# A two-layer graph network on one core: a fixed order ahead of the pairs, packed per-node scalars, and four blocks of counts kept as weights

## The chip, the cores and the metric

The kernel runs on one core of one Trainium2 chip. The metric is device time in microseconds, the median of several executions. The kernel before takes 452.44 us (three runs, 450.71 to 455.40); the profiled execution has a span of 452.8 us.

The core's engines are named as in the profile: PE is TensorE (matrix products), PEld its loading of weights, DVE is VectorE, ACT is ScalarE, POOL is GpSimd, SP only issues transfers.

## What is computed

`x` is 3327 x 64, `adj` is a symmetric 0/1 matrix of 3327 x 3327 with ones on its diagonal. Layer 0 works on every pair of nodes in hyperbolic space: for all i and j a logarithmic map of node j seen from node i, weighted by a sigmoid of two per-node logits and by the adjacency, summed over j; then per-node scalars, an exponential map and a projection. Layer 1 gives every edge the weight 0.5 to the power of the number of later edges in its row, for the last 100 edges of a row, and multiplies by a 64 x 64 weight.

```python
# layer 0, with h = relu(layernorm(x)); the result is added to x
x_t = logmap0(h, c)
left, right = x_t @ w_att[:D, 0], x_t @ w_att[D:, 0]
adj_att = sigmoid(left[:, None] + right[None, :] + b_att[0]) * adj
x_local = logmap(h[:, None, :], h[None, :, :], c)
support_t = einsum('ij,ijd->id', adj_att, x_local)
out = proj(expmap(h, support_t, c), c)
# layer 1, with h = relu(layernorm(x)) of the new x; the result is added to x
mask = adj != 0
rank = cumsum(mask, axis=1)
deg = rank[:, -1:]
k = minimum(deg, 100)
pos = rank - (deg - k)
w = mask * where(pos > 0, 0.5 ** (k - pos), 0)
out = w @ (h @ weight) + bias
```

The nodes are padded to 26 blocks of 128. The pairs are worked through in four strips of the i nodes (8, 8, 6 and 4 blocks wide); inside a strip a round is one block of j nodes (two blocks in the last strip), from the last j to the first. `NB` is 26, `P` 128, `D` 64.

## The kernel before

Ahead of the pairs, VectorE and ScalarE work out per-node scalars (`y`, `x2`, `nrm`, ...), features in float16 (`nz`, `nu`), their transposes (`jz`, `ju`) and the logits (`left`, `right`). The order of these instructions is left to a scheduler. All 26 blocks are transposed, in four groups:

```python
        for b0 in (24, 0, 16, 8):
            nb = min(8, NB - b0)
            for src, dst, rows in ((nu, ju, KB + 7), (nzf, jz, P)):
                pt = ps.tile([P, 8, P], F16, name="pq", bufs=2)
                for b in range(nb):
                    T.transpose(pt[:rows, b, :], src[:, b0 + b, :], id16)
                if dst is ju:
                    V.tensor_copy(dst[:rows, b0 : b0 + nb, :], pt[:rows, :nb, :])
                else:
                    A.copy(dst[:rows, b0 : b0 + nb, :], pt[:rows, :nb, :])
    ...
        for b in (*range(16, NB), *range(16)):
            for part in (0, 1):
                T.matmul(plr[:, b, :], jz[:, b, :], w_h[:, part], start=part == 0, stop=part == 1)
        V.tensor_mul(left, plr[:, :, 0], yr)
        V.tensor_mul(right, plr[:, :, 1], yr)
        V.tensor_scalar(right, right, batt, 0.5, op0=ALU.add, op1=ALU.mult)
    ...
        V.tensor_mul(hw[:, :, D], opx, wn)
        V.tensor_mul(wn, wn, y)
        for hs in node_halves[::-1]:
            V.tensor_mul(hw[:, hs, :D], rl[:, hs], wide(wn[:, hs], 13))
        V.tensor_mul(h, rl, wide(y, NB))
        V.tensor_scalar(balm, bal, MIN_NORM, None, op0=ALU.max)
        V.tensor_mul(su, nrm, balm)
        V.tensor_mul(sv, bal, su)
```

The pairs, whose order on TensorE, VectorE and ScalarE is that of the program:

```python
        queue = nc.scalar if k == 0 else nc.sync
        iz = strip.tile([P, 8, P], F16, name="iz")[:, :nb]
        iu = strip.tile([KB, 8, P], F16, name="iu")[:, :nb]
        queue.dma_start(iu[:D], ju[:D, blocks])
        queue.dma_start(iu[D:], ju[KB : KB + 7, blocks])
        queue.dma_start(iz[:D], jz[D:, blocks])
        queue.dma_start(iz[D:], jz[:D, blocks])
    ...
        kept = behind(j)[:, S.i0 : S.i0 + S.F]
        num, den = ON_ACT[k]
        i = NB - 1 - j
        if (n < AHEAD and k == 0) or i * num // den != (i + 1) * num // den:
            A.activation(kept, S.pc[:, : S.F], AF.Relu)
        else:
            V.tensor_scalar(kept, S.pc[:, : S.F], 0.0, None, op0=ALU.max)
    ...
    def strip_out(k):
        S = strips[k]
        S.ot = work.tile([P, FMAX], F32, name="sg", bufs=SGB)[: D + 1]
        V.tensor_copy(S.ot[:, : S.F], S.po[: D + 1, : S.F])
    ...
    steps = range_steps()
    strip_in(0)
    for n in range(AHEAD + 2):
        load(n)
    for n in range(AHEAD + 1):
        edges(n)
    for n in range(AHEAD):
        for j in js(n):
            count(n, j)
            read(n, j)
    with tc.manual_schedule(engines=IN_ORDER):
        products(0)
        for n in range(R):
            k, lo, hi = rounds[n]
            m, w = n + AHEAD, span(n)
            ended, turned = (n > i and rounds[n - i - 1][1] == 0 for i in (1, 2))
            if m + 2 < R:
                if rounds[m + 2][2] == NB:
                    strip_in(rounds[m + 2][0])
                load(m + 2)
            two = m < R and len(js(m)) == 2
            if two:
                count(m, js(m)[0])
            if turned:
                pa = turn(k - 1)
            elif n > 1:
                total(n - 2)
            pq = pq_of.pop(n)[:, :w]
            A.activation(pq, pq, AF.Gelu, scale=-WG / QS)
            A.activation(pq, pq, AF.Gelu, scale=WH)
            if n == 0:
                first_left()
                sigmoids(0)
            elif n == 1:
                left_to_dram()
            asked_of_act()
            if turned:
                steps = per_node(k - 1, pa)
            sg = sg_of[n][:, :w]
            V.scalar_tensor_tensor(sg, sg, 1.0, ad_of.pop(n)[:, :w], op0=ALU.add, op1=ALU.mult)
            if m + 1 < R:
                edges(m + 1)
            if two:
                read(m, js(m)[0])
            if m < R:
                count(m, js(m)[-1])
            if n + 1 < R:
                sigmoids(n + 1)
            if m < R:
                read(m, js(m)[-1])
            if n + 1 < R:
                products(n + 1)
            if hi - lo > 1:
                advance(PORTIONS[k])
            V.scalar_tensor_tensor(sg, pq, WD, sg, op0=ALU.add, op1=ALU.mult)
            if ended:
                strip_out(k - 1)
            advance(PORTIONS[k])
            if lo == 0:
                for _ in steps:
                    pass
                asked = False
            if turned:
                total(n - 2)
        total(R - 2)
        total(R - 1)
        strip_out(len(STRIPS) - 1)
        steps = per_node(len(STRIPS) - 1, turn(len(STRIPS) - 1))
```

`edges` makes a bfloat16 mask of the adjacency, `count` adds the edges behind every edge in PSUM, and `read` keeps these counts as bytes in `behind_lo` or `behind_hi`. `sigmoids`, `products` and `total` are the tanh of the logits, the pair products and the sum over j. The per-node tail of a strip (`post`) is a generator: in the first three strips its small instructions go to GpSimd, in the last to VectorE, and `yield` gives the share of a round that a step takes; `LATER` ends the round's share and `ACT` asks ScalarE for the next step. In the profile, L1064 and L1065 are the two Gelu of a round, L1075 the product with the adjacency, L1090 the final product, L974 a count read by VectorE, L1120 and L1122 the decodes of ScalarE and VectorE, and L849 the first large instruction that needs the tail's scalars (`V.tensor_mul(w, hs, ...)`). A shortened view of `post`:

```python
        def after(slots):
            for do, args, kwargs in asked_of_w:
                do(*args, **kwargs)
                if not hidden:
                    yield 1
            asked_of_w.clear()
            if not hidden:
                pass
            elif nb > 6:
                yield from [LATER] * slots
            else:
                yield from [LATER] * (slots + slots // 2)
        def root(y, v):
            t = small("rs_t")
            if hidden:
                W.tensor_tensor(y, v, nhalf[:, :nb], op=ALU.pow)
                W.tensor_mul(t, y, y)
                W.tensor_mul(t, t, v)
                W.tensor_scalar(t, t, -0.5, 1.5, op0=ALU.mult, op1=ALU.add)
                W.tensor_mul(y, y, t)
            else:
                rsqrt(W, pool, y, v, nb)
        ...
        A.activation(u, v, AF.Square)
        V.tensor_mul(dt, hs, v)
        yield BIG
        V.tensor_reduce(hv, dt, AX.X, ALU.add)
        yield BIG
        V.tensor_reduce(vv, u, AX.X, ALU.add)
        yield BIG
        muladd(sa, hv, m2c, agg[:, :, D])
        mul(sa, sa, su[:, bs])
        mul(xy, hv, sv[:, bs])
        mul(t0, sa, x2[:, bs])
        W.tensor_sub(xy, xy, t0)
        mul(u2, vv, sv[:, bs])
        mul(t0, sa, hv)
        W.tensor_sub(u2, u2, t0)
        mul(u2, u2, sv[:, bs])
        mul(t0, sa, xy)
        W.tensor_sub(u2, u2, t0)
        W.tensor_scalar(t0, u2, MIN_NORM, None, op0=ALU.max)
        root(rn, t0)
        mul(t0, t0, rn)
        mul(t0, t0, sk[:, bs])
        yield from after(2)
        yield ACT
        A.activation(k, t0, AF.Tanh)
        yield 0
        scaled(k, k, absr, rn)
        ...  # some 25 small instructions, one reciprocal, and a second root
        yield from after(4)
        V.tensor_mul(w, hs, wide(t0, nb))
        yield BIG
        ...  # 8 more large ones, and a third root
```

Layer 1 turns the counts, shifted by 7 bits, into bfloat16 weights by reading them as exponents (`decode`), and sums over j in seven PSUM banks:

```python
        def decode(j):
            wt = l1.tile([P, NP], U16, name="wt", bufs=7)
            if j % 2:
                A.activation(wt, behind(j), AF.Copy, scale=128.0)
            else:
                V.tensor_scalar(wt, behind(j), 128.0, None, op0=ALU.mult)
            return wt
        ...
        for j in range(late):
            wt = decode(j)
            asked_of_act()
            advance(LAST)
            if j == 8:
                in_range(l1_ps)
            for n in range(len(chunks)):
                add(j, wt, n)
            if j % 4 == 3:
                bias(j - 3, 4)
        for _ in steps:
            pass
        bias(late - 2, 2)
        bias(late, NB - late)
        weights = [decode(j) for j in range(late, NB)]
    ...
        for n in range(len(chunks)):
            for j in range(late, NB):
                add(j, weights[j - late], n)
            if n % 2:
                A.copy(ow[n], pw[n])
            else:
                V.tensor_copy(ow[n], pw[n])
            if n > 1:
                close(n - 2)
        close(len(chunks) - 2)
        close(len(chunks) - 1)
```

Of the kernel before, what the change touches and what calls it, by code (L numbers as in the profile page):

```python
# [22 lines left out]
P = 128  # L23
# [7 lines left out]
JH = 13  # L31
IN_ORDER = {mybir.EngineType.PE, mybir.EngineType.DVE, mybir.EngineType.Activation}
AHEAD = 3
SGB, ADB = 5, 7
# [3 lines left out]
PORTIONS, LAST = (2, 4, 4, 8), 8  # L38
BIG, LATER, ACT = 4, 99, 100

# [402 lines left out]
def fast(ctx, tc, x, adj_t, r, w_att, b_att, weight, bias, out, flag):  # L443
# [76 lines left out]
    def wide(t, n):  # L520
# [3 lines left out]
    h = const.tile([P, NB, D], F32, name="h")  # L524
    x2, bal, balm, nrm, left, right, sv, su, sk = (
        const.tile([P, NB], F32, name=n)
        for n in ("x2", "bal", "balm", "nrm", "left", "right", "sv", "su", "sk"))
# [4 lines left out]
    behind_hi = const.tile([P, NB - JH, NP], U8, name="behind_hi")  # L532
# [5 lines left out]
    pairs = ctx.enter_context(ExitStack())  # L538
    ps = pairs.enter_context(tc.tile_pool(name="ps", bufs=1, space=PSUM))

    with tc.tile_pool(name="pre", bufs=1) as pre:
        def small(name):
            return pre.tile([P, NB], F32, name=name)


        d, rl, sq, sr = (pre.tile([P, NB, D], F32, name=n) for n in ("d", "rl", "sq", "sr"))
        m, ss, rs, y, v = (small(n) for n in ("m", "ss", "rs", "y", "v"))
        for hs in node_halves:
            n = hs.stop - hs.start
            V.tensor_reduce(m[:, hs], x_sb[:, hs], AX.X, ALU.add)  # L550
            V.scalar_tensor_tensor(d[:, hs], wide(m[:, hs], n), -1.0 / D, x_sb[:, hs], op0=ALU.mult, op1=ALU.add)
            A.activation(sq[:, hs], d[:, hs], AF.Square)
            A.activation(rl[:, hs], d[:, hs], AF.Relu)
            A.activation(sr[:, hs], rl[:, hs], AF.Square)
        for hs in node_halves:
            V.tensor_reduce(ss[:, hs], sq[:, hs], AX.X, ALU.add)
            V.tensor_reduce(rs[:, hs], sr[:, hs], AX.X, ALU.add)
        V.tensor_scalar(v, ss, 1.0 / D, EPS_LN, op0=ALU.mult, op1=ALU.add)
        rsqrt(V, pre, y, v, NB)
        V.reciprocal(inv_r, r_c)  # L560
        V.tensor_mul(c_c, inv_r, inv_r)
        V.tensor_scalar(negc, c_c, -1.0, None, op0=ALU.mult)
        V.scalar_tensor_tensor(sqc, inv_r, -1.0, inv_r, op0=ALU.mult, op1=ALU.max)
        V.tensor_scalar(zs_c, sqc, ZS, None, op0=ALU.mult)
        V.tensor_scalar(za_c, c_c, -0.5 * ZS, None, op0=ALU.mult)

# [659 lines left out]
```

## Time and profile before

| engine | busy us | share of the span | instructions |
|---|---|---|---|
| TensorE | 371.7 | 82% | 1438 |
| VectorE | 383.3 | 85% | 579 |
| ScalarE | 371.5 | 82% | 410 |
| GpSimd | 95.7 | 21% | 231 |

| stage | us from the span's start |
|---|---|
| first final product of a pair round (L1090) starts | 50.2 |
| strip 1's first L1090 | 140.9 |
| strip 2's first L1090 | 239.7 |
| strip 3's first L1090 | 327.3 |
| last sums of the pairs copied (L1004) | 385.1 |
| last decode of layer 1 ends | 434.4 |
| last VectorE instruction ends | 445.4 |

No engine is full over the whole span, and three are close to it together; so the shares say little, and the stages have to be read one by one. Times of waits are what an engine stood idle before an instruction, put down to what released it last.

### The profile page before, as it was taken

Reading aid. Unit: us, or ns where it says so; the run is one execution under the profiler, and the core shown is the slowest. Engines: PE = TensorE matmul, PEld = TensorE weight load, DVE = VectorE, ACT = ScalarE, POOL = GpSimd, SP = SyncE. Lnnn points to the kernel's source line nnn. Section 1 sums busy time; section 2 is a strip of 40 time slices with the busy share of each in tenths; the row PEclk is TensorE's granted clock in tenths of the full one; section 3 lists DMA queues with packets and bytes.
Section 4 is the critical chain, followed back from the end, with each engine's and each line's share of the span. In section 5 each row is a group of like instructions: output and inputs, shape, how many; then the busy total and the mean of one; then the engine's idle time right before and its main releaser. Section 6 shows DMA issues by size and latency. Waiting matters only on the chain.

```text
span 452.8 us, 4738 instructions
## 1 busy us (share of the span) xinstructions
PE 371.7 (82%) x1438; PEld 159.3 (35%) x1460; DVE 383.3 (85%) x579; ACT 371.5 (82%) x410; POOL 95.7 (21%) x231
## 2 busy tenths in 40 slices
PE   0436899999997999989997999697979958768963
PEld 0124333333333333333333444343333312323443
DVE  3893799999999899799999686999999776989821
ACT  1645999999999899979998799699998946893940
POOL 5000000000000257702400468023026812000000
PEclk9997799999999899989998899699999979899997
DMA  8503344544547345344345353336534000000002
GB/s 194 211 1 73 121 159 140 167 154 144 157 142 226 109 147 165 94 139 137 106 125 162 83 150 117 96 114 186 160 120 139 0 0 0 1 1 0 1 23 60
DMA packets 23313, 48.98 MB, mean 108 GB/s; under 512 B 8714, under 2 KB 9170, under 8 KB 23280
## 3 DMA queue, kind: packets, MB, share of 16 engines
q1 hardware_dynamic: 20993, 47.66, 35.0%
q10 hardware_dynamic: 2062, 0.87, 1.0%
q0 software_dynamic: 224, 0.07, 0.3%
q8 instruction: 13, 0.21, 0.2%
q14 instruction: 21, 0.16, 0.1%
HBM read 46.40 MB, written 0.87 MB: 104 GB/s over the span
## 4 chain that ended last, share of the span: by engine, by line


## 5 line engine op out<-in xcount | busy, mean ns | idle before, releaser
L998 PE MATMUL po<-sg,hw 128*65 128x512 f32 (+1 forms) x364 | 164.2, 576 | 1.6 <-DVE sg L1090 1.5
L1090 DVE SCALAR_TENSOR_TENSOR sg<-pq,sg 128x1024 f32<-128x1024 f32 (+1 forms) x91 | 103.7, 1139 | 8.6 <-ACT pq L1065 8.3
L1075 DVE SCALAR_TENSOR_TENSOR sg<-sg,ad 128x1024 f32<-128x1024 f32 (+1 forms) x91 | 103.7, 1139 | 7.0 <-ACT sg L981 6.7
L981 ACT ACTIVATE sg<-left_b,right 128x1024 f32<-128x1024 f32 (+2 forms) x104 | 100.5, 980 | 0.0
L1064 ACT ACTIVATE pq<-pq 128x1024 f32<-128x1024 f32 (+1 forms) x91 | 87.1, 957 | 7.1 <-PE pq L989 6.2
L1065 ACT ACTIVATE pq<-pq 128x1024 f32<-128x1024 f32 (+1 forms) x91 | 86.2, 947 | 2.9
L961 PE MATMUL pc<-mask,ca 128*128 128x512 bf16 (+1 forms) x169 | 64.8, 383 | 24.4 <-DVE behind_lo L974 11.7
L998 PEld LDWEIGHTS po<-sg,hw 128*65 128x65 f32 x364 | 50.8, 141 | 74.5 <-issue 60.8
L962 PE MATMUL pc<-mask,cb 128*128 128x512 bf16 (+1 forms) x170 | 63.9, 385 | 15.9 <-DVE mask L950 13.9
L989 PE MATMUL pq<-iz,jz 128*128 128x512 f16 (+1 forms) x182 | 67.9, 379 | 4.0 <-DMA iz<-jz 4.0
L988 PE MATMUL pq<-iu,ju 71*128 71x512 f16 (+1 forms) x182 | 69.5, 382 | 1.0 <-DVE sg L1090 0.3
L950 DVE TENSOR_SCALAR mask<-ad 128x1024 bf16<-128x1024 f32 (+1 forms) x91 | 59.2, 652 | 0.6 <-PE pc L961 0.6
L1127 PE MATMUL pw<-wt,s 128*128 128x512 bf16 (+1 forms) x178 | 41.7, 383 | 9.2 <-DVE wt L1122 5.5
L962 PEld LDWEIGHTS <-cb 128*128 128x128 bf16 x182 | 18.5, 101 | 78.5 <-issue 61.6
L755 POOL TENSOR_SCALAR sa<-hv,m2c 128x8 f32<-128x8 f32 (+1 forms) x3 | 3.0, 1004 | 201.5 <-ACT behind_hi L972 147.9
L972 ACT ACTIVATE behind_lo<-pc 128x1024 uint8<-128x1024 f32 (+2 forms) x32 | 27.4, 855 | 12.2 <-PE pc L962 6.8
L972 ACT ACTIVATE behind_hi<-pc 128x1024 uint8<-128x1024 f32 (+2 forms) x31 | 27.0, 871 | 8.1 <-PE pc L962 8.1
L1127 PEld LDWEIGHTS <-s 128*128 128x128 f16 x182 | 18.4, 103 | 30.5 <-issue 13.0
L961 PEld LDWEIGHTS <-ca 128*128 128x128 bf16 x175 | 17.9, 102 | 30.6 <-issue 19.5
L989 PEld LDWEIGHTS <-jz 128*128 128x128 f16 x182 | 18.6, 102 | 24.8 <-issue 4.5
L988 PEld LDWEIGHTS <-ju 71*128 71x128 f16 x182 | 18.6, 102 | 24.6 <-DVE sg L1090 4.7
L1132 POOL TENSOR_TENSOR x_sb<-x_sb,bias_b 128x256 f32<-128x256 f32 (+1 forms) x7 | 7.2, 1042 | 79.5 <-DVE w L860 79.5
(265 smaller groups left out, 346.6 us busy)
## 6 DMA issues: line engine op xcount, KB each, us to landing
ad<-in_adj_t SPq DMA_DIRECT2D x65, 512.0 KB, 3.6
ad<-in_adj_t SPq DMA_DIRECT2D x26, 384.0 KB, 3.2
out<-o SPq DMA_DIRECT2D x6, 128.0 KB, 2.6
left_b<-left_d SPq DMA_DIRECT2D x1, 512.0 KB
x_sb<-in_x ACTq DMA_DIRECT2D x1, 416.0 KB, 5.7
x_sb<-in_x SPq DMA_DIRECT2D x1, 416.0 KB, 5.1
left_b<-left_d SPq DMA_DIRECT2D x1, 384.0 KB, 4.2
iz<-jz SPq DMA_DIRECT2D x2, 128.0 KB, 2.7
```

Of the source, the lines that this page charges most:

```text
L950: V.tensor_scalar(*args, 0.0, None, op0=ALU.not_equal)
L961: T.matmul(S.pc[:, f0:f1], ca, S.before[:, f0:f1], start=False, stop=True, skip_group_check=True)
L962: T.matmul(S.pc[:, f0:f1], cb, now[:, f0:f1], start=S.first, stop=True, skip_group_check=True)
L981: A.activation(part(n, sg, j), S.left[:, : S.F], AF.Tanh, bias=right[:, j : j + 1], scale=0.5)
L988: T.matmul(part(n, pq, j, f0, f1), ju[:KB, j, :], S.iu[:, f0:f1], start=True, stop=False)
L989: T.matmul(part(n, pq, j, f0, f1), jz[:, j, :], S.iz[:, f0:f1], start=False, stop=True)
L998: T.matmul(S.po[: D + 1, f0:f1], hw[:, j, :], part(n, sg_of[n], j, f0, f1), start=j == NB - 1, stop=j == 0)
L1064: A.activation(pq, pq, AF.Gelu, scale=-WG / QS)
L1065: A.activation(pq, pq, AF.Gelu, scale=WH)
L1075: V.scalar_tensor_tensor(sg, sg, 1.0, ad_of.pop(n)[:, :w], op0=ALU.add, op1=ALU.mult)
L1090: V.scalar_tensor_tensor(sg, pq, WD, sg, op0=ALU.add, op1=ALU.mult)
L1127: T.matmul(pw[n], s2[:, j].rearrange("p c d -> p (c d)"), wt[:, f0:f1].bitcast(BF16), start=j == 0, stop=j == NB - 1)
```

## The change

It has five parts.

1. *A fixed order ahead of the pairs.* The part ahead of the loop also gets a written order on TensorE, VectorE and ScalarE. The blocks that the first rounds need (0 to 7 and 24, 25) are transposed first, the first strip's regrouping transfers are issued by SP and GpSimd, not ScalarE, and what is needed later (the other blocks, the weights `hw`, scalars of the tail) moves into the first two rounds. Two rounds are counted ahead, not three, and there are five adjacency buffers, not seven.
2. *Packed per-node scalars.* In the tail, scalars that go through the same operation are neighbours in one tile, so that one instruction does both; `h` is no longer kept (`hw` times a per-node factor `ih` stands in). The last strip's roots take a power on GpSimd in place of three refinement steps on VectorE. The waiting steps are given as times and divided by a round's length (`ROUND`).
3. *Counts kept as weights.* Blocks 12 to 15 (`JD`) are written by `read` as 16-bit weights at once and need no decode; layer 1 begins with them.
4. *One decode ahead.* The first decode is asked for ahead of the last strip's tail; a tail that isn't done at the end of its strip goes on in the next stage.
5. *The range test in the loop.* The test that decides whether the general path must run moves from layer 1 into the last two rounds. The copy of a strip's sums is split between VectorE and ScalarE, and stands ahead of the round's final product.

The diff, cut to its core:

```diff
-JH = 13
+JD = range(12, 16)
 IN_ORDER = {mybir.EngineType.PE, mybir.EngineType.DVE, mybir.EngineType.Activation}
-AHEAD = 3
-SGB, ADB = 5, 7
+AHEAD = 2
+SGB, ADB = 5, 5
 ON_ACT = ((1, 2), (5, 8), (3, 4), (1, 2))
-PORTIONS, LAST = (2, 4, 4, 8), 8
+PORTIONS, LAST = (2, 4, 4, 8), 6
 BIG, LATER, ACT = 4, 99, 100
+ROUND = (3.5, 3.5, 2.8, 1.9)
...
+    for n in range(AHEAD + 2):
+        load(n)
+    pairs.enter_context(tc.manual_schedule(engines=IN_ORDER))
...
+    first_i, last_j, later = slice(0, 8), slice(24, NB), slice(8, 24)
...
+    p1 = ps.tile([P, 16, P], F16, name="pq", bufs=2)
+    turned_to(p1, first_i, 0)
+    p2 = ps.tile([P, 4, P], F16, name="po")
+    turned_to(p2, last_j, 0)
+    kept(p1, first_i, 0)
+    strip_in(0)
+    kept(p2, last_j, 0)
+    p3 = ps.tile([P, 16, P], F16, name="pq", bufs=2)
...
+    logits((first_i, last_j))
+    products(0)
+    rest(later)
+    high, low = slice(16, 24), slice(8, 16)
+    turned_to(p3, high, 0)
+    pl = first_left()
+    products(1)
+    edges(AHEAD)
+    pq = pq_of[0]
+    A.activation(pq, pq, AF.Gelu, scale=-WG / QS)
+    A.activation(pq, pq, AF.Gelu, scale=WH)
+    kept(p3, high, 0)
+    strips[0].left, left_b = pl, strips[0].left
+    sigmoids(0)
+    A.copy(left_b[:, : strips[0].F], pl[:, : strips[0].F])
+    strips[0].left = left_b
...
+    def last_of_ahead():
+        p4 = ps.tile([P, 16, P], F16, name="po")
+        turned_to(p4, low, 0)
+        kept(p4, low, 0)
         wn, opx = small("wn"), small("opx")
         V.tensor_scalar(wn, nrm, WA / 2, None, op0=ALU.mult)
         V.tensor_scalar(opx, x2, c_c, 1.0, op0=ALU.mult, op1=ALU.add)
         V.tensor_mul(hw[:, :, D], opx, wn)
         V.tensor_mul(wn, wn, y)
-        for hs in node_halves[::-1]:
-            V.tensor_mul(hw[:, hs, :D], rl[:, hs], wide(wn[:, hs], 13))
-        V.tensor_mul(h, rl, wide(y, NB))
+        V.tensor_mul(hw[:, 13:, :D], rl[:, 13:], wide(wn[:, 13:], 13))
+        yield
+        logits((later,))
+        left_to_dram()
+        yield
+        V.tensor_mul(hw[:, :13, :D], rl[:, :13], wide(wn[:, :13], 13))
+        V.tensor_scalar(ih, babs, 2 / WA, None, op0=ALU.mult)
...
+            A.activation(kept, S.pc[:, : S.F], AF.Relu, scale=128.0 if j in JD else 1.0)
+        elif j in JD:
+            V.tensor_scalar(kept, S.pc[:, : S.F], 0.0, 128.0, op0=ALU.max, op1=ALU.mult)
...
+        other = nc.gpsimd if k == 0 else nc.sync
+        iz = strip.tile([P, 8, P], F16, name="iz")[:, :nb]
+        iu = strip.tile([KB, 8, P], F16, name="iu")[:, :nb]
+        other.dma_start(iz[:D], jz[D:, blocks])
+        nc.sync.dma_start(iz[D:], jz[:D, blocks])
+        other.dma_start(iu[:D], ju[:D, blocks])
+        nc.sync.dma_start(iu[D:], ju[KB : KB + 7, blocks])
...
+        def power(y, v, exponent):
+            asked_of_w.append((G.tensor_tensor, (y, v, exponent[:, :nb]), {"op": ALU.pow}))
+        def root(y, v):
+            power(y, v, nhalf)
+            mul(rt, y, y)
+            if hidden:
+                mul(rt, rt, v)
+                W.tensor_scalar(rt, rt, -0.5, 1.5, op0=ALU.mult, op1=ALU.add)
+                mul(y, y, rt)
+            else:
+                W.scalar_tensor_tensor(rt, v, -0.5, rt, op0=ALU.mult, op1=ALU.mult)
+                W.scalar_tensor_tensor(y, rt, 1.5, y, op0=ALU.add, op1=ALU.mult)
...
+                    yield LATER if kwargs.get("op") == ALU.pow else 1
             asked_of_w.clear()
-            if not hidden:
-                pass
-            elif nb > 6:
-                yield from [LATER] * slots
-            else:
-                yield from [LATER] * (slots + slots // 2)
-        def root(y, v):
-            t = small("rs_t")
             if hidden:
-                W.tensor_tensor(y, v, nhalf[:, :nb], op=ALU.pow)
-                W.tensor_mul(t, y, y)
-                W.tensor_mul(t, t, v)
-                W.tensor_scalar(t, t, -0.5, 1.5, op0=ALU.mult, op1=ALU.add)
-                W.tensor_mul(y, y, t)
-            else:
-                rsqrt(W, pool, y, v, nb)
-        hs, v, xs = h[:, bs], agg[:, :, :D], x_sb[:, bs]
-        sa, t0, t1, k, y2, u2, xy, hv, vv, rn = (
-            small(n) for n in ("sa", "t0", "t1", "k", "y2", "u2", "xy", "hv", "vv", "rn"))
-        u, w, dt = big("u"), big("w"), big("dt")
+                yield from [LATER] * math.ceil(time / ROUND[k + 1])
...
+        mul(d, dots[:, 1:], both(of_sum[:, 1]))
+        mul(e, dots[:, :2], both(of_sum[:, 0]))
+        W.tensor_sub(d, d, e)
+        mul(e, d, of_sum)
+        W.tensor_sub(d[:, 1], e[:, 1], e[:, 0])
...
-        V.tensor_copy(S.ot[:, : S.F], S.po[: D + 1, : S.F])
+        for f0, f1 in S.hv:
+            if f0 == 0:
+                V.tensor_copy(S.ot[:, f0:f1], S.po[: D + 1, f0:f1])
+            else:
+                A.copy(S.ot[:, f0:f1], S.po[: D + 1, f0:f1])
...
+        if ended:
+            strip_out(k - 1)
+        if 0 < n < R - 1:
...
+        if n > R - 3:
+            next(range_end)
...
+    order = [*JD, *range(JD.start), *range(JD.stop, late)]
...
+            nonlocal decoded
+            if j in JD:
+                return behind(j)
             wt = l1.tile([P, NP], U16, name="wt", bufs=7)
-            if j % 2:
+            decoded += 1
+            if decoded % 2:
...
+        weights = {j: decode(j) for j in order[: len(JD) + 1]}
+        stages.append(Stage(per_node(len(STRIPS) - 1, pa)))
...
```

## The prediction

> **What bounds the kernel now.** The chain that ended last is empty on this page, so I read stage by stage: first the busy time of each engine in stretches, cut where the strips change.
>
> ```profile
> core 0: us, PE busy (x) PEld busy (x) DVE busy (x) ACT busy (x) POOL busy (x), PEclk, DMA share, GB/s
> 0.00:50.00 50.00, 18.19 (x134) 11.72 (x136) 31.01 (x103) 24.99 (x30) 6.57 (x26) 0.93 0.38 109
> 50.00:140.00 90.00, 89.27 (x301) 33.95 (x306) 89.86 (x100) 88.43 (x91) 0.00 (x0) 0.98 0.53 162
> 140.00:239.00 99.00, 92.41 (x312) 35.44 (x316) 92.92 (x101) 93.46 (x101) 34.77 (x68) 0.97 0.45 133
> 239.00:327.00 88.00, 77.06 (x313) 36.33 (x316) 76.95 (x103) 78.29 (x106) 29.08 (x68) 0.92 0.45 132
> 327.00:385.00 58.00, 47.34 (x146) 16.99 (x147) 46.72 (x56) 45.52 (x65) 24.55 (x68) 0.94 0.19 55
> 385.00:435.00 50.00, 37.38 (x164) 16.79 (x167) 40.79 (x110) 39.10 (x18) 0.73 (x1) 0.93 0.00 1
> ```
>
> The stretches are the front, strips 0 to 3, and layer 1 up to its last decode; the close takes the remaining 18 us. Strip 0 is full: VectorE 89.9 of 90 us, ScalarE 88.4. There a round takes 2.87 us on VectorE without a count read and 4.00 with one, 3.43 on average, and nothing short of less work helps. Strips 1, 2 and 3 leave VectorE idle for 6, 11 and 11 us, layer 1 for 9. The list of waits for VectorE says what ended most of that:
>
> ```profile
> DVE w L849 <- POOL t L755: 11.2, 3, 4.4
> DVE sg L1090 <- ACT pq L1065: 8.3, 12, 1.9
> DVE sg L1075 <- ACT sg L981: 6.7, 1, 6.7
> ```
>
> The first line is the per-node tail: in each of strips 1 to 3 VectorE stops once, for 3.2, 3.6 and 4.4 us, for scalars that GpSimd is still working out. The third is the first round, which waits for the chain ahead of the pairs. In the timeline of VectorE and then in four stretches after it, the third GpSimd wait shows what it costs besides itself:
>
> ```profile
> 363.45 0.56 DVE L849 TENSOR_TENSOR w<-h,t 128x384 f32<-128x384 f32 x1 [4.36 <-POOL t L755]
> ```
>
> ```profile
> 366.00:370.00 4.00, 1.32 (x3) 0.56 (x4) 3.93 (x7) 0.49 (x1) 0.46 (x1) 0.75 0.00 0
> 370.00:374.00 4.00, 4.00 (x7) 1.24 (x6) 2.04 (x3) 2.86 (x5) 0.68 (x2) 0.50 0.00 0
> ```
>
> TensorE has 1.3 us of work in one stretch, and in the next it runs with a granted clock of 0.50. In layer 1 the timeline of ScalarE shows which decodes come last:
>
> ```profile
> 405.26 2.96 ACT L1120 ACTIVATE wt<-behind_hi 128x3328 uint16<-128x3328 uint8 x1
> 413.99 0.42 ACT L863 ACTIVATE dt<-w 128x256 f32<-128x256 f32 x1 [5.76 <-DVE w L860]
> 414.31 2.96 ACT L1120 ACTIVATE wt<-behind_hi 128x3328 uint16<-128x3328 uint8 x1
> 419.61 0.40 ACT L874 CAST s<-w 128x256 f16<-128x256 f32 x1 [2.34 <-DVE w L871]
> 419.92 14.44 ACT L1120 ACTIVATE wt<-behind_hi 128x3328 uint16<-128x3328 uint8 x5
> ```
>
> Thirteen decodes of 2.9 us sit on ScalarE, which stops 5.8 and 2.3 us for the last strip's per-node work on VectorE and ends at 434.4. TensorE's last 28 products need that decode, so the 11 us of closing begin there.
>
> [...] a wait of 5.3 us, then clock 0.50. [...] here GpSimd's 128x8 scale took 0.20 to 0.28 us in some places and 1.75 in others[...]. [...] a 128x4 product takes 0.16 us here and 128x256 takes 0.42, so packing two 128x4 products into one saves almost all of one. [...]
>
> **The change part by part.**
>
> *Front.* Before, the first final product (L1090) starts at 50.16. The chain that sets it: features at 25.6, transposed and copied in four groups up to 37.9, the DMA regrouping of the first strip issued from 32.8 but landed only at 42.7 (half of it sits in ScalarE's queue behind copies and the table load), then the activations. The change transposes just the needed ten blocks first and moves those DMAs to two other queues. Walking the new program order with the durations of this page: x can start at about 6.5 (before it waited behind the r scalars until 8.2), per-node scalars end at 21, the first features at 22.5, transposes at 27, DMA landed at 31, first products at 33. But `left` needs the logarithms (32.4), and its transposes stand in TensorE's order behind a group that waits for the later blocks (38), so the first tanh is at 40.5 and the first L1090 at about 44: 6 us sooner. Against that stand postponed items, now in rounds 0 and 1, where VectorE has no room: two weight copies of 0.95, one ju copy 0.6, and some twenty small ones of about 0.15: 5 us. The 1.9 us `h` product disappears, but it was ahead. I book a net -2.
>
> *One look-ahead less.* Two rounds counted ahead instead of three: one mask (0.6) and half of a read (1.14) move into full rounds, +1.
>
> *GpSimd's scalars.* Packed chains are shorter (the middle one has 33 instructions for 38, and it took 19 us before), and slots are now sized by time: 16 us at 3.5 us a round gives 5 rounds where 4 were waited. In strips 2 and 3 it is 6 and 9 steps for 4 and 6. I expect all 11.2 us to go. All of it is on the path, because VectorE and ScalarE are both full between the strips.
>
> *After the third wait.* With TensorE warm, the last four rounds need not take 17.4 us (364.40 to 381.84 between L1090s); ScalarE's floor for a round without a count is 3.2 us (375.68 to 378.86), 12.8 for four: -4.
>
> *Strip ends.* The copy of the sums is issued before L1090 (1.14 us earlier) and halved with ScalarE. TensorE waited 2.8 us plus 2.5 us for it at two strip ends and 0.8 at the last, and VectorE 1.3 and 1.9 behind that: -3.
>
> *Layer 1.* TensorE needs 26 x 6.5 x 0.213 us = 36 us at full clock (its start-to-start distance is about 0.21), so the decodes and the last strip's scalars bind. Two decodes fewer per engine: 3.6 us of VectorE (1.81 start to start), 5.8 of ScalarE. The range test leaves (1.6 us). Small VectorE instructions fall from 76 to 46: at some 0.17 us each, 5. Back come three GpSimd powers of 1.35 us, half covered by a decode (+3), and the rest of strip 2's post that no longer ends inside strip 3 (5 large instructions, +2.5). VectorE was packed from 385.75 to 428.9, 43 us: 43 - 3.6 - 1.6 - 5 + 3 + 2.5 = 38. ScalarE needs 11 x 2.9 plus 2.5 = 34.5 and again waits for VectorE. Its last decode, 49 us after the pairs before, should come at 41: -8. I don't take the 12 us that TensorE's own floor would allow.
>
> Sum: -2 + 1 - 11.2 - 4 - 3 - 8 = -27, and 452.4 - 27 = 425.
>
> **Rivals.** (1) *The front gives nothing or costs.* A fixed order loses what the scheduler filled in; the postponed work meets full engines. For it: strip 0 has no slack. Against it: 6.7 us of idle VectorE ahead of the first round. That makes 430 or so. (2) *A load wait takes the place of the GpSimd wait.* Seven adjacency buffers become five, so from release to use there are two rounds, 6.9 us, not three. A load lands in 3.6 us, but at each strip's start 0.9 MB of regrouped features stand in front of it in the same queue. Against it: the DMA share is 0.5 and no load wait shows now. If it binds, about 1 to 3 us at three places: 428 to 434. (3) *Layer 1 stays bound by the chain through VectorE,* with GpSimd's powers put into it: then that part gives 3 and not 8, 430. (4) *Better:* TensorE's floor in layer 1 is reached and the front chain is shorter than I walked it: 414.
>
> **Range and chances.** The certain core is the 11 us of GpSimd waits and the two decodes per engine; 9 us, the 2% line, is less than the first alone. Front and layer 1 are each uncertain by 5 or 6 us, the strip ends by 3, together about 9. So 425, 413 to 440; faster 0.91, same 0.06, slower 0.03.
>
> **What would show it.** The wait of L849's successor on GpSimd near zero; L1090's first start near 44, and rounds 0 to 2 longer than 4 us; no granted clock near 0.5 in strip 3; the last decode about 41 us after the pairs end. Wrong would be: VectorE waiting for loads at strip starts, a first L1090 later than 48, or ScalarE still pausing 8 us in layer 1.

## The result and the profile after

| | before | after |
|---|---|---|
| time, median of four executions | 452.62 us (450.71 to 455.40) | 436.23 us (435.56 to 436.67) |
| ratio, 95% interval | | 0.963 (0.958 to 0.968) |
| span of the profiled execution | 452.8 us | 434.5 us |

So 16.4 us were gained, and 27 had been booked: 436.2 lies in the range, 11 us above the 425 of the prediction. Between the two profiles it is 18.3, because the profiled execution of the kernel before took 454.5 us, 2 us above its median; the differences between stages below contain these 2 us. First the stages of the kernel after, with the cuts moved to its own strips; columns as in the same view of the kernel before.

```profile
core 0: us, PE busy (x) PEld busy (x) DVE busy (x) ACT busy (x) POOL busy (x), PEclk, DMA share, GB/s
0.00:45.00 45.00, 14.12 (x98) 8.66 (x98) 28.10 (x87) 22.79 (x29) 8.49 (x30) 1.00 0.32 90
45.00:142.00 97.00, 92.12 (x343) 35.63 (x344) 95.90 (x122) 91.28 (x93) 0.19 (x1) 0.96 0.52 158
142.00:237.00 95.00, 91.46 (x317) 34.70 (x315) 91.61 (x100) 92.44 (x100) 35.13 (x62) 0.98 0.46 140
237.00:317.00 80.00, 72.42 (x313) 34.28 (x312) 73.70 (x101) 76.80 (x104) 33.41 (x62) 0.98 0.48 138
317.00:374.00 57.00, 48.83 (x155) 17.44 (x153) 49.40 (x66) 48.52 (x66) 22.58 (x52) 0.94 0.25 74
374.00:415.00 41.00, 33.34 (x163) 15.69 (x163) 33.18 (x74) 31.44 (x17) 11.60 (x11) 1.00 0.00 1
```

The front is 5 us shorter (45 for 50), but strip 0 is 7 us longer (97 for 90), strips 1 and 2 are 4 and 8 us shorter, strip 3 hardly. VectorE is again full in strip 0 and idle for 3, 6 and 8 us in strips 1 to 3. In its list of waits, what was first is gone and two waits are new (the final product is now L1173, the product with the adjacency L1154, the decodes L1205 and L1207, a strip's aggregates, its sums turned back to one node per partition, are copied half by L1098 on ScalarE and half by L1100 on VectorE, where before ScalarE copied both halves; the large product that needs the tail's scalars is L1045):

```profile
DVE agg L1100 <- ACT agg L1098: 5.7, 3, 2.0
...
DVE w2s L1190 <- DMA w<-in_weight: 4.2, 1, 4.2
DVE rt_last L967 <- POOL rn_last L967: 2.7, 3, 0.9
...
DVE w L1067 <- POOL rn L967: 0.5, 1, 0.5
```

No line has L1045: the 11.2 us of waits for GpSimd have become 0.5 (L1067, a later step of the tail), and in layer 1 three short waits for the new powers come to 2.7. New is the first line: three times, once in each of strips 1 to 3, VectorE's half of the aggregates' copy waits about 2 us for ScalarE's half, and stands ahead of everything VectorE would do next. At the start of strip 3 this is what follows, in the timeline of TensorE and in the two stretches around it:

```profile
328.29 0.59 PE L629 MATMUL pc<-mask,ca 128*128 128x512 bf16 x1 [4.19 <-DVE behind_hi L644]
```

```profile
325.00:329.00 4.00, 0.71 (x2) 0.25 (x2) 3.35 (x6) 1.80 (x4) 0.00 (x0) 0.76 0.14 19
329.00:333.00 4.00, 4.00 (x8) 1.39 (x7) 3.69 (x5) 2.93 (x4) 2.97 (x8) 0.50 0.32 116
```

VectorE reads a count late, TensorE waits 4.2 us for the free buffer, and then runs at a granted clock of 0.50 (called cold below). The four rounds there take 5.28, 6.73, 6.10 and 4.50 us; the kernel before took 3.67, 5.39, 3.94 and 3.90 in its own. Layer 1 on ScalarE:

```profile
369.05 2.97 ACT L1205 ACTIVATE wt<-behind_lo 128x3328 uint16<-128x3328 uint8 x1
374.77 0.38 ACT L1098 COPY agg_last<-po 128x260 f32<-128x260 f32 x1 [2.75 <-PE po L1088]
...
380.05 0.51 ACT L1070 CAST s<-w 128x384 f16<-128x384 f32 x1 [4.17 <-DVE w L1067]
...
405.50 0.40 ACT L1070 CAST s<-w_last 128x256 f16<-128x256 f32 x1 [3.05 <-DVE w_last L1067]
405.81 8.70 ACT L1205 ACTIVATE wt<-behind_hi 128x3328 uint16<-128x3328 uint8 x3
```

The last decode (the end of the last line) is at 414.5, 41.0 us after the last copy of the sums begins (373.53; before it was 49.2), though ScalarE pauses for 11.0 us on the way (2.75, 4.17, 3.05 in these lines, 0.63 and 0.41 in others).

Cut at the first final product of each strip, the two profiles give this account; the booked terms are the prediction's.

| stage | before | after | booked | found |
|---|---|---|---|---|
| start to strip 1 | 140.89 | 141.87 | -2 + 1 | +1.0 |
| strip 1 | 98.77 | 95.27 | | -3.5 |
| strip 2 | 87.63 | 80.06 | | -7.6 |
| strip 3, to its last final product | 54.55 | 53.08 | | -1.5 |
| strips 1 to 3 together | | | -11.2 - 4 - 3 | -12.5 |
| last final product to last decode | 52.52 | 44.24 | -8 | -8.3 |
| last decode to the end | 18.41 | 19.96 | 0 | +1.5 |

Layer 1 is as booked. Missing are 5.7 us in the strips, 2 in the front and 1.5 in the closing. The experiments ask for each.

### The profile page after: what moved, and what is told of

Read it like the earlier page. It is cut to its first block, busy times and chain, and to the rows that moved or that the text cites. A ratio compares the mean times of both kernels' runs of the same rounds, so it can differ in the third digit from the quotient of the medians.

```text
span 434.5 us, 4704 instructions
## 1 busy us (share of the span) xinstructions
PE 364.4 (84%) x1460; PEld 155.8 (36%) x1460; DVE 377.1 (87%) x556; ACT 365.0 (84%) x409; POOL 111.4 (26%) x218
## 4 chain that ended last, share of the span: by engine, by line
DVE 38%; ACT 23%; PE 22%; issue 10%; POOL 3%; DMA 2%; POOLq 0%; DVEq 0%; ACTq 0%
DVE sg L1173 11%; DVE sg L1154 10%; PE po L668 8%; ACT sg L651 6%; ACT pq L1147 5%; DVE behind_lo L644 3%; ACT pq L1148 3%; PE pc L629 2%; PE pq L658 2%; PE pq L659 2%; PE pc L630 2%; DVE wt L1207 2%; ACT wt L1205 2%; DVE behind_hi L644 2%; ACT behind_lo L640 2%
## 5 line engine op out<-in xcount | busy, mean ns | idle before, releaser
L668 PE MATMUL po<-sg,hw 128*65 128x512 f32 (+1 forms) x364 | 161.1, 566 | 0.4 <-DVE st L895 0.4
L1173 DVE SCALAR_TENSOR_TENSOR sg<-pq,sg 128x1024 f32<-128x1024 f32 (+1 forms) x91 | 103.8, 1140 | 6.6 <-ACT pq L1148 5.3
L1154 DVE SCALAR_TENSOR_TENSOR sg<-sg,ad 128x1024 f32<-128x1024 f32 (+1 forms) x91 | 103.9, 1142 | 2.5 <-ACT sg L651 2.4
L651 ACT ACTIVATE sg<-left_b,right 128x1024 f32<-128x1024 f32 (+2 forms) x103 | 99.5, 978 | 1.0 <-DVE right L819 1.0
L1147 ACT ACTIVATE pq<-pq 128x1024 f32<-128x1024 f32 (+1 forms) x90 | 86.1, 957 | 4.4 <-PE pq L659 4.3
L1148 ACT ACTIVATE pq<-pq 128x1024 f32<-128x1024 f32 (+1 forms) x90 | 85.2, 946 | 2.9
L630 PE MATMUL pc<-mask,cb 128*128 128x512 bf16 (+1 forms) x182 | 66.9, 378 | 16.3 <-DVE mask L618 14.8
L668 PEld LDWEIGHTS po<-sg,hw 128*65 128x65 f32 x364 | 49.5, 138 | 70.1 <-issue 55.1
L1218 PE MATMUL pw<-wt,s 128*128 128x512 bf16 (+1 forms) x154 | 33.9, 371 | 7.4 <-DVE wt L1207 5.1
L967 POOL TENSOR_TENSOR dots<-dots,ih 128x8 f32<-128x8 f32 (+1 forms) x3 | 2.6, 876 | 141.1 <-DVE dots L987 141.1
L658 PEld LDWEIGHTS <-ju 71*128 71x128 f16 x182 | 18.2, 100 | 23.9 <-DVE sg L1173 5.2
L640 ACT ACTIVATE behind_hi<-pc 128x1024 uint8<-128x1024 f32 (+2 forms) x24 | 20.7, 864 | 7.1 <-PE pc L630 7.1
L659 PEld LDWEIGHTS <-jz 128*128 128x128 f16 x182 | 18.4, 101 | 19.9 <-issue 3.5
L640 ACT ACTIVATE behind_lo<-pc 128x1024 uint8<-128x1024 f32 (+2 forms) x29 | 24.9, 858 | 0.0
L1223 POOL TENSOR_TENSOR x_sb<-x_sb,bias_b 128x256 f32<-128x256 f32 (+1 forms) x6 | 9.9, 1660 | 49.6 <-DVE w L1056 44.0
```

What stands on the lines that cost most here:

```text
L630: T.matmul(S.pc[:, f0:f1], cb, now[:, f0:f1], start=S.first, stop=True, skip_group_check=True)
L640: A.activation(kept, S.pc[:, : S.F], AF.Relu, scale=128.0 if j in JD else 1.0)
L651: A.activation(part(n, sg, j), S.left[:, : S.F], AF.Tanh, bias=right[:, j : j + 1], scale=0.5)
L658: T.matmul(part(n, pq, j, f0, f1), ju[:KB, j, :], S.iu[:, f0:f1], start=True, stop=False)
L659: T.matmul(part(n, pq, j, f0, f1), jz[:, j, :], S.iz[:, f0:f1], start=False, stop=True)
L668: T.matmul(S.po[: D + 1, f0:f1], hw[:, j, :], part(n, sg_of[n], j, f0, f1), start=j == NB - 1, stop=j == 0)
```

## The experiments

Every time is a median of four or five executions, and every ratio is to the kernel before on the same chip. Three chips were used, on which the kernel before takes 452.6 to 453.2 us, so half a microsecond between two of the runs says nothing. The theory was that the 5.7 us of the strips lie in the split copy of the aggregates, and the 2 us of the front in the wait for `in_weight`; the rival was that both waits are slack.

**The aggregates' copy on one engine.** In the kernel after:

```diff
-            if c == 0:
-                A.copy(to, of)
-            else:
-                V.tensor_copy(to, of)
+            A.copy(to, of)
```

> The changed kernel, with both copies of the turned sums on ScalarE again, as before the change. Theory: the copy that VectorE got stands ahead of the round's first product and waits for ScalarE's copy, 1.8 + 2.0 + 1.9 us at the three strip ends, and at the last one it also makes TensorE wait 4.2 us and run at half clock. Then this run gains those 5.7 us and 2 to 4 of what follows: 427 to 430 for 436.2. Rival: the slow start of strip 3 comes from the half of the sums that ScalarE copies, or from strip 1's tail that runs over into strip 3; then the wait only moves and the time stays within 2 us of 436.

Measured: 432.64 us, 0.956 (0.951 to 0.961), 3.6 us less. In strip 3, TensorE's wait and the same two stretches became:

```profile
327.29 0.38 PE L629 MATMUL pc<-mask,ca 128*128 128x512 bf16 x1 [1.98 <-DVE behind_hi L644]
```

```profile
325.00:329.00 4.00, 2.02 (x12) 0.94 (x11) 3.97 (x6) 3.97 (x9) 0.53 (x2) 1.00 0.42 127
329.00:333.00 4.00, 4.00 (x13) 1.41 (x12) 4.00 (x6) 3.23 (x5) 3.25 (x9) 1.00 0.21 50
```

No cold clock, and strip 3 takes 48.10 us in place of 53.08. Strips 1 and 2 did not move by 0.1 us (95.31 and 80.11). So the theory holds in strip 3 alone, for 5.0 us; 1.1 of them are lost again ahead of it, since strip 1 starts that much later in this profile than in that of after, in code that the edit does not touch. In the other two strips the rival holds: VectorE, no longer kept by the copy, now waits for a count (2.9 us in one place), because TensorE is late. What makes it late is asked further down. All the kernels here bear the 5 us out: strip 3 takes 52.0 to 53.4 us in the four with the split copy (that with the short waiting, below, left out), 48.1 to 48.4 in four of those without it, and 49.8 in the other three, which the last section is about.

**The scaled weight late.** In the kernel after, `w2s` had no place in the fixed order. Its scheduler put it third on VectorE, where it waited 4.2 us for a transfer while the node features stood behind it. The edit writes it late in layer 1:

```diff
     w2s = const.tile([P, D], F32, name="w2s")
-    V.tensor_scalar(w2s, w2, 2.0**27 / HS, None, op0=ALU.mult)
     late = STRIPS[-1][0]
...
         finish()
+        V.tensor_scalar(w2s, w2, 2.0**27 / HS, None, op0=ALU.mult)
         bias(STRIPS[-2][0], late - STRIPS[-2][0])
```

> The changed kernel, with the scaling of layer 1's weight written late in VectorE's fixed order; in the changed kernel it was left to the scheduler, which put it third on VectorE, where it waits 4.2 us for a small transfer. Theory: that wait is on the front's chain, so the first final product starts at 41 and not 45 and the time falls by 3 to 4 us. Rival: the masks behind it need the adjacency loads, which land at about the same time; then it falls by less than 1.5 us.

Measured: 433.67 us, 0.958 (0.954 to 0.962), 2.6 us less; the first final product starts at 42.91 and not 45.16. A little under the theory, well over the rival: the wait was on the path, but only 2.3 of its 4.2 us arrive there. The timeline of VectorE shows why, first of the kernel after, then of this one:

```profile
13.01 0.20 DVE L1190 TENSOR_SCALAR w2s<-w 128x64 f32<-128x64 f32 x1 [4.16 <-DMA w<-in_weight]
```

```profile
12.33 0.69 DVE L618 TENSOR_SCALAR mask<-ad 128x1024 bf16<-128x1024 f32 x1 [1.82 <-DMA ad<-in_adj_t]
```

With the wait for `in_weight` gone, a mask behind it waits 1.8 us for its load of the adjacency. So the rival named the right wait, and it takes over less than half.

**Both, and three decodes ahead.**

```diff
-        weights = {j: decode(j) for j in order[: len(JD) + 1]}
+        weights = {j: decode(j) for j in order[: len(JD) + 3]}
```

> Both edits together, and three decodes ahead of the last strip's tail, not one. Theory: layer 1 is bound by ScalarE, which stands 2.7 and 4.2 us ahead of its second decode; with a decode more there, its last decode comes 3 us sooner after the pairs. With e1 and e2 that makes 436 - 8 - 3.5 - 3 = 421 to 424. Rival: VectorE binds layer 1 and its decode ahead delays the tail by 1.8 us; then no better than e1 and e2 added.

Measured: 427.97 us, 0.946 (0.942 to 0.950), 4 us more than the upper end of what was expected, mostly because 8 us were counted for the first edit, which brought 3.6. This is the combined kernel of what follows. From last final product to last decode it is 42.8 us, 1.5 less than after and not 3. No load is late in the rounds, so nothing here shows the prediction's second rival; the one wait for a load is that of the mask in the front (1.7 us here).

**Longer waiting alone, packing alone.** Two runs separate the two parts that aim at GpSimd's scalars. The first is the kernel before, with 5, 6 and 9 waiting steps ahead of the large product in place of 4, 4 and 6:

```diff
+            elif slots == 4:
+                yield from [LATER] * {0: 5, 8: 6, 16: 9}[b0]
```

> The kernel before the change, with nothing but longer waits ahead of the large instructions that need GpSimd's scalars: 5, 6 and 9 steps for 4, 4 and 6. Theory: the 11.2 us of VectorE's waits for GpSimd were on the path in full and longer waiting alone removes them: 452.5 falls to 440 to 443, and TensorE stays warm in strip 3. Rival: the large instructions then no longer fit in their strip, are flushed at its end and wait there; then it stays above 446.

Measured: 443.3 us, 0.981 (0.976 to 0.985). The waits ahead of the large product are gone; a wait of 2.1 us for the last root remains. Strips 1, 2 and 3 are shorter by 3.0, 3.7 and 7.9 us; the waits taken away were 3.2, 3.6 and 4.4. Of the 3.6 us beyond the wait in strip 3, 2.7 are in the last four rounds, at the place of the cold stretch behind the third wait: 14.7 us, for 17.4 before, at a mean clock of 0.80. These are two single profiles, though: this one is of the shortest of its four executions (441.42 us), and that of before is 2 us above its median. By the medians 9.3 us are gained, and some 10.9 in the strips if layer 1, which took 1.6 more, is taken out: that is the waits, and no more.

The second is the kernel after with the waiting steps of the kernel before:

```diff
-                yield from [LATER] * math.ceil(time / ROUND[k + 1])
+                yield from [LATER] * {8.5: (2, 2, 3), 16: (4, 4, 6), 6: (2, 2, 3)}[time][k]
```

> The kernel after (436.2 us) with the number of waiting steps put back to that of the kernel before (2, 4, 2 in strips 1 and 2, 3, 6, 3 in strip 3), so that the packed scalars alone have to remove VectorE's wait for GpSimd. Theory: packing alone does not do it; 33 instructions for 38 shorten the long chain by a seventh or so (19 us to 16.5), so of the waits of 3.2, 3.6 and 4.4 us some 1 to 2 us each remain, with a cold TensorE after the third: 439 to 442 us. Rival: the packed chain is short enough for the old steps and the longer waiting was not needed: 435 to 437 us, waits of L1045 on GpSimd under 1 us in all.

Measured: 443.77 us, 0.978 (0.974 to 0.982), 7.5 us more than after. The list of waits for VectorE begins with

```profile
DVE w L1045 <- POOL of_end L967: 7.6, 3, 3.7
```

The three waits are 0.55, 3.33 and 3.69 us where the kernel before had 3.20, 3.63 and 4.36: packing helps in strip 1 and hardly in the others, and the cold TensorE is back (clock 0.50 for 3.4 us after a wait of 5.2 us). The theory holds, and the remainder is larger than it said. It is the longer waiting that removes the 11.2 us; packing alone would have left two thirds of them.

**No kept weights.** The kernel after, with all 26 blocks decoded:

```diff
-JD = range(12, 16)
+JD = range(13, 13)
```

> The kernel after (436.2 us) with the kept layer 1 weights alone undone: no block is kept ready, all 26 are decoded in layer 1, alternating between the engines. Theory (the prediction's step): two decodes more on each engine, 5.8 us of ScalarE's time, and TensorE cannot start at once: last decode some 5 to 6 us later, 441 to 443 us. Rival: the decodes were not what bound layer 1, the last strip's per-node chain was, and ScalarE, which stood idle for 10 us there, fills its pauses with them: 436 to 439 us.

Measured: 440.18 us, 0.971 (0.967 to 0.975), 4.0 us more; between the two profiles the last decode comes 3.1 us later after the last final product (47.3 for 44.2). It lies between theory and rival. ScalarE's pauses show why: they fall from 11.0 to 8.5 us, so of two more decodes on ScalarE, 5.8 us, 2.5 go into time in which it stood idle, and 3.3 are paid.

**The last strip's roots on VectorE.** The kernel after:

```diff
         def root(y, v):
+            if not hidden:
+                rsqrt(W, pool, y, v, nb)
+                return
             power(y, v, nhalf)
```

> The kernel after (436.2 us) with the last strip's three roots back on VectorE (11 small instructions each, three Newton steps) in place of GpSimd's power and one Newton step. Theory: the three powers (1.4 to 2.6 us each, only partly covered by a decode) cost about what they save, so the last decode moves by less than 1.5 us: 435 to 438 us. Rival A: VectorE's waits for them (2.7 us in all) lie on the path, so it gains 2 to 3 us: 433 to 434 us. Rival B: 8 more small instructions per root at 0.17 to 0.2 us all lie on the path: plus 3 to 4 us, 439 to 441 us.

Measured: 438.80 us, 0.968 (0.964 to 0.971). That would be 2.6 us more, but this run's front was late: its strip 1 starts 2.1 us later than after, in code that the edit does not touch. From last final product to last decode it is 44.8 us for 44.2. In that stage the theory holds: the powers neither cost nor bring much.

**Who makes TensorE late at strip ends 1 and 2.** In the combined kernel TensorE waits 1.85 us for ScalarE's half of the copied sums before it can transpose them. Here VectorE copies both halves:

```diff
-            if f0 == 0:
-                V.tensor_copy(S.ot[:, f0:f1], S.po[: D + 1, f0:f1])
-            else:
-                A.copy(S.ot[:, f0:f1], S.po[: D + 1, f0:f1])
+            V.tensor_copy(S.ot[:, f0:f1], S.po[: D + 1, f0:f1])
```

> The combined kernel (both aggregate copies on ScalarE, w2s late, three weights ahead; 427.97 us) with one more edit: both halves of the copy of the sums stay on VectorE, at the early place. In the kernel after, TensorE's turn waited 1.85 us at each of two strip ends for ScalarE's half. Theory: that wait goes and little comes back, since VectorE then stood waiting for the count anyway: 1 to 2 us at each of two strip ends, 424 to 426.5 us. Rival: VectorE pays for each whole copy what TensorE gains (some 0.6 us more at each of four strip ends), so halving the copy with ScalarE was right: 427.5 to 430 us.

Measured: 427.53 us, 0.943 (0.939 to 0.947), the same as 427.97 within the intervals; strips 1 and 2 take 95.30 and 79.80 us. TensorE waits 1.85 and 1.50 us there, now for VectorE. The time is that of the rival: who copies hardly matters. So the next edit gives TensorE something to do in the wait:

```diff
+        if turned and not two:
+            count(m, js(m)[-1])
         if turned:
             pa = turn(k - 1)
...
-        if m < R:
+        if m < R and (two or not turned):
             count(m, js(m)[-1])
```

> The combined kernel (427.97 us) with one more edit: in the round of a turn of sums (strip ends 1 and 2, where rounds have one source block) the counts of two rounds ahead are put before the transposes in TensorE's order. In that kernel TensorE stood idle 1.85 us for ScalarE's half of the copy of the sums, and 4.0 us of sums in the next stretch then delayed the counts, for which VectorE waited 2.9 us. Theory: TensorE's wait is what starts that delay, the counts can fill about 0.9 us of it and shorten the cold stretch behind it; 1 to 2 us less at each of two strip ends, 424 to 426.5 us. Rival: TensorE is full in these strips (3.7 us of work per round of 3.5 us), or the count has to wait itself for the read ahead of it, so the delay only moves: 427 to 428.5 us.

Measured: 425.11 us, 0.938 (0.934 to 0.941). Strips 1 and 2 take 93.93 and 78.85 us, 1.4 and 1.3 less than in the combined kernel. TensorE's timeline at strip end 1 has two short waits for the one of 1.85:

```profile
143.61 0.38 PE L629 MATMUL pc<-mask,ca 128*128 128x512 bf16 x1 [1.17 <-ACT behind_hi L640]
...
146.81 3.65 PE L668 MATMUL po<-sg,hw 128*65 128x512 f32 x8 [0.81 <-ACT agg L1097]
```

They add up to more, 1.98 us, and the work around them is the same, but the clock behind them is another. The same two stretches, first of the combined kernel, then of this one:

```profile
145.00:147.00 2.00, 2.00 (x13) 0.93 (x12) 2.00 (x4) 1.97 (x4) 0.00 (x0) 0.67 0.35 141
147.00:149.00 2.00, 2.00 (x5) 0.69 (x4) 2.00 (x3) 2.00 (x4) 0.00 (x0) 0.50 0.80 231
```

```profile
145.00:147.00 2.00, 1.19 (x7) 0.45 (x6) 2.00 (x3) 1.97 (x5) 0.00 (x0) 1.00 0.32 90
147.00:149.00 2.00, 2.00 (x5) 0.55 (x4) 2.00 (x3) 2.00 (x3) 0.00 (x0) 1.00 0.74 256
```

So the theory holds, with one correction: with as much idle time and the same work, what the edit saves is the stretch at 0.67 and 0.50 that followed the one long wait.

**The pauses of ScalarE in layer 1.** Two edits try to fill them. One gives ScalarE 12 of the 22 decodes, the extra one where it pauses; it was run on the combined kernel and on the one just above.

```diff
-            if decoded % 2:
+            if decoded in (1, 3, 4, 6, 8, 10, 12, 14, 15, 17, 19, 21):
```

> The combined kernel (427.97 us) with another share of the decodes in layer 1: ScalarE decodes 12 of 22 and not 11, the fourth and the fifteenth on it, just where it stood idle for 4.5 us and 3.1 us; VectorE decodes 10. Theory: layer 1 is bound by the last strip's per-node chain through VectorE, which now comes 1.85 us sooner, while ScalarE fills its pause: last decode 1.5 to 3 us sooner, 425 to 426.5 us. Rival: ScalarE's own sum of decodes (35 us of the 42) is the bound by now, and the decode added to it is paid in full or the pauses move: 427 to 430 us.

> Both edits together on the combined kernel (427.97 us): counts ahead of the transposes, and 12 of 22 decodes on ScalarE. They touch different stages, so the theory is that their gains add: 422 to 425 us. Rival: either gains nothing: 425.5 to 428 us.

Measured: 429.94 us, 0.948 (0.944 to 0.952), and 427.03 us, 0.941 (0.938 to 0.945): 2.0 and 1.9 us more than without the edit. The rival holds, in layer 1. The first pause stayed at 4.5 us, since it waits for VectorE's chain and not for work, the next became 3.6, and the last decode came 43.7 us after the last final product in both, not 42.8. That is 0.9 us; the rest of the loss is in the closing, 20.2 us for 18.0 in the first and 18.4 for 17.6 in the second, of which more below. The gain of the counts' edit is the same with it and without.

The other keeps 11 decodes on ScalarE but puts three of them at the start:

```diff
-            if decoded % 2:
+            if decoded < 4 or 4 < decoded < 20 and decoded % 2:
```

> The kernel with counts ahead of the transposes (425.11 us) with one more edit: ScalarE still decodes 11 of 22 blocks in layer 1, but the first three instead of the first, the third and so on to the last but one, so that a decode stands in its pause of 4.5 us and VectorE comes to the per-node work 1.9 us sooner. Theory: in the run with 12 decodes on ScalarE the share was what cost, not the order; with the share kept, filling the pause moves ScalarE's last decode by 1.5 to 3 us, until VectorE's own last decode (1.4 us before ScalarE's in that kernel) is the last: 423 to 424.5 us. Rival: the pause comes back elsewhere, or the products wait for the later decodes that VectorE now has at the end: 425 to 427 us.

Measured: 429.22 us, 0.947 (0.940 to 0.955), 4.1 us more than the 425.11 of the kernel it was made from. The four executions fall into pairs, 427.3 and 427.8, 430.7 and 430.8, and the profile is of the longer pair. The rival holds, in a form that it didn't name: VectorE now waits.

```profile
DVE t L1061 <- ACT u L1059: 4.2, 1, 4.2
```

The square of strip 2's tail stands behind the three decodes on ScalarE, VectorE's chain needs it, and its last decode ends 45.7 us after the last final product, 2.9 later than without the edit. The closing, 19.7 us for 17.6, adds 2.1 in this profile. ScalarE's pause is the price of its being there when the chain calls.

The best kernel of these is the one with 425.11 us: the kernel after with the aggregates copied by ScalarE, `w2s` late, three decodes ahead and the counts before the transposes. It beats both kernels.

## Why the gain was 11 us less than predicted

*Front, booked -2.* The terms of the prediction itself, 6 us sooner and 5 us of postponed work, make -1. The walk gave 44 us for the first final product, and it was 45.2; rounds 0 and 1 then took 6.2 and 6.8 us where they had taken 4.5 and 3.2, 5.3 us more where 5 were booked. At round 2 the kernels stand at 58.2 and 57.9: +0.3. The term was mis-sized because the walk followed the program's order and did not see that an instruction written outside it would be put third on VectorE. Taking it out brought 2.3 us at the first final product and 2.6 in the time. The agreement on the 5 us is partly luck: in nine kernels with this front TensorE waits 3.2 to 3.8 us for the postponed copy of `jz` and 1.7 us for the postponed logits, and in the kernel after it runs for 6.8 us at a clock of 0.50 around them, from 47.2 to 54.0. Round 1 took 6.8 to 8.2 us in kernels whose code is the same up to there.

*One look-ahead less, booked +1.* From round 2 to strip 1 the kernel after needs 83.7 us, before 83.0. It agrees, though no run isolates it.

*GpSimd's waits, booked -11.2, and the cold stretch behind the third, booked -4.* The first holds: the waits went from 11.2 to 0.5. The reason given was two-fold, packing and slots; the runs show that the slots were needed, with packing alone 7.6 us of waits stay. The second has the mechanism right and the size wrong: the last four rounds ran at a clock of 1.00, but took 15.4 us where 12.8 had been said, so that it brought 2.0 and not the booked 4. None of them was as short as the 3.2 us that were counted for each (3.67 to 4.27).

*Strip ends, booked -3.* This is the step that failed. It counted the copy of the sums, earlier and halved, and not that the next copy on the way, that of the aggregates, was now also halved between two engines, in a place where VectorE stands and waits for the slower half. With that copy on ScalarE alone, the three strips take 17.4 us less than before, where 11.2, 4 and 3 had been booked, 18.2 in all; with it split, 12.5. The 5.0 between the two are all in strip 3. What the step had promised came in small part: TensorE's waits for the copy of the sums at strip ends 1 and 2 were 2.3 and 2.5 us (the prediction's 2.8 is that of its weight loading), and are 1.9 each. "No granted clock near 0.5 in strip 3" was to show the step before right; there was one, of 0.50, behind this other wait. The 0.50 followed a wait of 4.2 us; waits of 1.9 us at strip ends 1 and 2 of the same kernel were followed by 0.50 too, for 3.4 us each.

*Layer 1, booked -8, found -8.3, and the last decode 41 us after the pairs, as said.* Yet its reasons were only half seen. The kept weights are worth 3.1 us there and not the 3.6 of VectorE or 5.8 of ScalarE that they take away, the powers next to nothing; by subtraction, the rest comes from the packed chain, the decode ahead and the range test, which no run isolates. The sign named for a failure, ScalarE pausing for 8 us, came (11.0) without the failure: the pauses were slack against VectorE's chain.

*The closing, not booked,* took 20.0 us for 18.4. Its code did not change but for the place of `w2s`. After the last decode TensorE's first ten products took 3.22 us, and eight took 2.10 before; the mean clock of the first 5.5 us was 0.69, and 1.00 before. Of the five kernels with just this closing, two took 18.4 and 18.5 us and three 19.8 to 20.4, so I don't put it down to the change.

Of the rivals, the first came true (the front gave nothing). The second came in no run: no load was late from round 0 on. The third fell. The loss at strip 3 was in none of them.

## What to carry to other kernels

When a copy is split between two engines that work in a written order, look at what stands behind each half: here the half that waited for the other held up what stood after it, and the loss showed one engine further on, as a wait of 4.2 us and a clock of 0.50 on TensorE. It need not: of three such waits of 1.8 to 2.0 us one cost 5 us, and two cost nothing, since the same engine then waited for something else. Give every instruction a place once an order is written by hand, for one that is left out can land ahead of the chain with a transfer in front of it, as `w2s` did here for 4.2 us; and before such a wait is taken out, look at the next one behind it, which here took 1.8 of them. Before an engine's pause is filled, ask whom it is waiting for and who will then call it: of three attempts to fill ScalarE's pauses one brought the last decode 1.5 us forward, and two put it 0.9 and 2.9 us back.

## What was not expected of the hardware

A gap of 1.98 us in TensorE's work, at the same place in strip 3 and with the same work around it, left the clock at 1.00 in three kernels (among them the first experiment above) and took it to 0.50 in two others, the one with counts ahead of the transposes (for 3.4 us) and the one with three decodes first. The two stretches behind the gap, first of the combined kernel, where it ends at 324.78, then of the one with counts ahead, where it ends at 321.73:

```profile
325.00:327.00 2.00, 2.00 (x9) 0.85 (x8) 1.97 (x4) 2.00 (x5) 0.87 (x4) 1.00 0.65 234
327.00:329.00 2.00, 2.00 (x7) 0.69 (x6) 2.00 (x3) 1.97 (x3) 1.74 (x4) 1.00 0.04 8
```

```profile
322.00:324.00 2.00, 2.00 (x7) 0.86 (x6) 1.97 (x4) 1.53 (x4) 0.92 (x4) 0.55 0.68 240
324.00:326.00 2.00, 2.00 (x4) 0.47 (x3) 2.00 (x3) 1.90 (x2) 1.74 (x4) 0.60 0.03 8
```

That cost the second 1.7 us against the first (49.8 us for 48.1 in strip 3). The kernel with both counts ahead and 12 decodes on ScalarE has the same gap and takes 49.8 us too. The closing has a pair like it: the kernels before and after both wait 2.27 us for the last decode, and behind it the clock stayed at 1.00 in the first and was 0.50 from 415.8 to 419.3 in the second.

So a gap of 1.98 us, and one of 2.27, were followed by 1.00 in one case and by 0.50 in another. What decides between them was not shown: no run moved a gap on purpose to test it.
